# Four chunks of the first experts beside the head softmax instead of two, the projections in halves, and the openings normalized on ACT

## The chip, the cores and the metric

The kernel runs on one core of a Trainium2 chip. The metric is the device time of one execution in microseconds (us). All arithmetic is in 32-bit floating point. PE is TensorE, DVE is VectorE, ACT is ScalarE, POOL is GpSimd, and SP issues most of the DMAs.

## The reference

The input x is 2 batches of 1024 tokens of width 128. Eight residual steps follow, each `x = x + f(layernorm(x))` with its own f. The first five (a latent attention, a spiking feed-forward network, a state space, the spiking network again, a linear attention) lie ahead of the change. The last three are what matters here:

```python
x = x + experts(layernorm(x))
x = x + head_softmax_attention(layernorm(x))   # softmax over the 16 heads, not over the keys
x = x + experts(layernorm(x))

def experts(x):            # 8 experts, hidden 512, each applied to every token
    for wg, wu, wd in zip(Wg, Wu, Wd):
        acc = acc + (silu(x @ wg) * (x @ wu)) @ wd

def head_softmax_attention(x):                 # 16 heads of width 8
    dp = einsum('bhqd,bhkd->bhqk', q, k) * 8 ** -0.5
    attn = softmax(dp, axis=1)                 # axis 1 is the head
    out = einsum('bhqk,bhkd->bhqd', attn, v) @ w_proj + b_proj
```

Both expert steps use the same weights.

## The kernel before

The tokens stay in SBUF as `x_res`, 16 tiles of 128 tokens; batch 0 has tiles 0 to 7, batch 1 tiles 8 to 15. There are two forms of the experts.

- `experts_ffn(chunks)` takes chunks of 512 tokens (4 tiles). Its units, 8 experts x 4 slices of the hidden width, run as a pipeline: products (two 128x512 matmuls), gate on ACT (Silu), multiplication on DVE, and the output matmul two units later into one PSUM bank.
- `ExpertStream` takes chunks of 256 tokens (2 tiles), numbered 0 to 7, also 32 units each, and is fed step by step: `products` takes two units, `gates` applies Silu, `multiply` forms `e_h`, `outputs` multiplies two of these with `Wd` into a bank `h_pd`, and `add` adds it to `x_res`. An `opening` normalizes a chunk (statistics on DVE, root on ACT, inverse on DVE, apply, transposes on PE) and so makes its 32 units available. Two units handled by one call are called a pair below.

`heads_and_experts(first, second)` computes the attention and weaves the stream into it: the chunks `first` are still the experts ahead of the attention, and `second` those behind it. It runs under a manual schedule: each engine does its instructions in the order in which they are written.

- `preparation(b)` makes queries, keys and values of a batch, as steps that name the engine they belong to ("dve", "act", "pool", "pe").
- 128 blocks follow: for each batch, 8 query tiles x 8 key tiles of 128. A block computes the scores of all 16 heads (`products`, h_s), the maximum over the heads (DVE, h_m), the difference (DVE, h_e), the exponential (ACT), the sum over the heads (a copy of half of h_e by a DMA from SP, an accumulating DMA from POOL, and eight matmuls with the identity, h_pd), the reciprocal (DVE, h_r), the weights (POOL, h_a) and the weighted values (PE, h_po). These run skewed over several turns of one loop. The score banks (`h_s`) and `h_pd` exist once.
- In each turn the stream gives one pair: outputs, multiplication, products and gates stand at fixed places between the steps of the softmax.
- `aside(place)` does one waiting step of a side list if it belongs to that engine. A "pe" step takes the place of the products of that turn. The side list says when an opening or a preparation may start: at so many finished query tiles, and with at most so many units left.
- Ahead of the blocks, the steps of `preparation(0)` alternate with pairs of the stream's first chunk; behind the last block the rest of the stream is done alone.

At the end of the kernel the calls are

```python
    experts_ffn(g, w, [2])
    heads_and_experts(g, w, [6, 7], [0, 1, 2, 3, 4, 5])
    experts_ffn(g, w, [3])
```

Tiles 8 to 11 of batch 1 are the 512-token chunk 2, or the stream's chunks 4 and 5. `experts_ffn([3])` is the second expert step of the last four tiles.

Of the kernel before, what the change touches and what calls it, by code (L numbers as in the profile page):

```python
# [9 lines left out]
F32 = mybir.dt.float32  # L10
BF16 = mybir.dt.bfloat16
AF = mybir.ActivationFunctionType
# [7 lines left out]
P = 128  # L20
B = 2
L = 1024
D = 128
NT = B * L // P
TPB = L // P
# [975 lines left out]
class ExpertStream:  # L1001
# [5 lines left out]
    def __init__(self, g, w, work, ps):  # L1007
        self.g, self.w, self.work, self.ps = g, w, work, ps
        self.units, self.fresh, self.gated, self.ready, self.sums = [], [], [], [], []

    def tokens(self, chunk):
        return self.g.x[:, 2 * chunk : 2 * chunk + 2, :]

    def opening(self, chunk):

        g, nc = self.g, self.g.nc
        ln = StagedNorm(g, self.tokens(chunk), 2, "ex")
        u = self.work.tile([P, 2, D], F32, name="e_u", bufs=1)
        yield "dve", lambda: ln.stats(range(2))
        yield "act", ln.root  # L1020
        yield "dve", ln.inverse
        yield "pool", lambda: ln.apply(u, range(2))

        def transposes():
            pt = self.ps.tile([P, 4, P], F32, name="e_pgu")
            for t in range(2):
                nc.tensor.transpose(pt[:, t, :], u[:, t, :], g.ident)
            uT = self.work.tile([P, 2 * P], F32, name="e_uT")
            nc.scalar.copy(uT, pt[:, 0:2, :].rearrange("p a b -> p (a b)"))
            self.units += [(chunk, e, fc, uT) for e in range(self.NE) for fc in range(self.FC)]  # L1030

        yield "pe", transposes

# [58 lines left out]
def heads_and_experts(g, w, first, second):  # L1092

    nc, tc = g.nc, g.tc
    J, K, HD, H = 4, 4, 8, 16
    scale = HD**-0.5
    with ExitStack() as es:
        pool = lambda name, bufs, **kw: es.enter_context(tc.tile_pool(name=name, bufs=bufs, **kw))
        one = pool("h_one", 1)
        seq = pool("h_seq", 2)  # L1100
# [19 lines left out]
        vz = one.tile([P, TPB * J, K, K, HD], F32, name="h_vz")  # L1120
        nc.gpsimd.memset(vz, 0.0)
        ex = ExpertStream(g, w, ework, ps_e)
        qzs, kTs, vs = {}, {}, {}

        def preparation(b):

            xb = g.x[:, b * TPB : (b + 1) * TPB, :]
            ln = StagedNorm(g, xb, TPB, "h")
            u = seq.tile([P, TPB, D], F32, name="h_u", bufs=1)
            uT = seq.tile([P, L], F32, name="h_uT", bufs=1)  # L1130
            qzs[b] = seq.tile([P, K, L], F32, name="h_qz")
            kTs[b] = seq.tile([P, L], F32, name="h_kT")
            vs[b] = seq.tile([P, TPB, D], F32, name="h_v", bufs=1)
            for t in range(0, TPB, 2):
                yield "dve", lambda t=t: ln.stats((t, t + 1))
            yield "act", ln.root
            yield "dve", ln.inverse
            for t in range(0, TPB, 2):
                yield "pool", lambda t=t: ln.apply(u, (t, t + 1))


            def bias(t):
                nc.gpsimd.tensor_add(
                    xb[:, t : t + 4, :], xb[:, t : t + 4, :], w["b_proj2"].unsqueeze(1).to_broadcast([P, 4, D])
                )

            def transposes(n):
                pt = ps_e.tile([P, 4, P], F32, name="e_pgu")
                for t in range(4):
                    nc.tensor.transpose(pt[:, t, :], u[:, 4 * n + t, :], g.ident)  # L1150
                nc.scalar.copy(uT[:, bass.ts(n, 512)], pt.rearrange("p a b -> p (a b)"))

            def query(n):
                cols = bass.ts(n, 512)
                pm = ps_e.tile([P, 4, P], F32, name="e_pgu").rearrange("p a b -> p (a b)")
                nc.tensor.matmul(pm, w["w_qkv2"][:, 0:P], uT[:, cols], start=True, stop=True)
                for k in range(K):
                    nc.scalar.activation(  # L1158
                        qzs[b][:, k, cols], pm, AF.Identity, bias=keep_b[:, k : k + 1], scale=keep[:, k : k + 1]
                    )  # L1160

            def key(n):
                cols = bass.ts(n, 512)
                pm = ps_e.tile([P, 4, P], F32, name="e_pgu").rearrange("p a b -> p (a b)")
                nc.tensor.matmul(pm, w["w_qkv2"][:, P : 2 * P], uT[:, cols], start=True, stop=True)
                nc.scalar.activation(kTs[b][:, cols], pm, AF.Identity, bias=w["b_qk2"][:, 1:2])

            def value(n):
                pv = ps_e.tile([P, 4, P], F32, name="e_pgu")
                for t in range(4):  # L1170
                    nc.tensor.matmul(
                        pv[:, t, :], uT[:, bass.ts(4 * n + t, P)], w["w_qkv2"][:, 2 * P : 3 * P], start=True, stop=True
                    )
                nc.vector.tensor_add(
                    vs[b][:, 4 * n : 4 * n + 4, :], pv, w["b_v2"].unsqueeze(1).to_broadcast([P, 4, D])
                )

            for step in (transposes, key, query, value):
                for n in range(2):
                    yield "pe", lambda step=step, n=n: step(n)  # L1180
            for t in (0, 4):
                yield "pool", lambda t=t: bias(t)

        def spread(b):
            v = vs[b].rearrange("p t (j k d) -> p (t j) k d", j=J, k=K)
# [2 lines left out]

        def products(b, qb, kb):

            s = ps_s.tile([P, J, 512], F32, name="h_s")
            for j in range(J):
                quad = slice(32 * j, 32 * j + 32)
                nc.tensor.matmul(  # L1194
                    s[:, j, :].rearrange("p (k q) -> p k q", k=K),
                    kTs[b][quad, bass.ts(kb, P)],
                    qzs[b][quad, :, bass.ts(qb, P)],
                    start=True,
                    stop=True,
                )  # L1200
            return s.rearrange("p j (k q) -> p (j k) q", k=K)
# [50 lines left out]

        side = [(2 * c + 2, 8, ex.opening(c)) for c in second]
        side.insert(1, (0, 24, preparation(1)))
        side = [(0, 8, ex.opening(c)) for c in first[1:]] + side
        finished, current, head = 0, None, None

        def aside(place):  # L1260

            nonlocal current, head
            while True:
                if head is None:
                    if current is None:
# [12 lines left out]
            return True  # L1278

# [5 lines left out]
        n = len(blocks)  # L1285
        with tc.manual_schedule(engines=ALL):
            for _, step in ex.opening(first[0]):
                step()
            for place, step in preparation(0):
                step()  # L1290
                if place != "act":
                    po = ps_d.tile([P, 4, D], F32, name="h_pd")
                    ex.outputs(po)
                    ex.add()
                    ex.products()
                    ex.gates()
                    ex.multiply()
            spread(0)
            e_, e2_, d_, a_ = {}, {}, {}, {}
            oT = po = None  # L1300
# [159 lines left out]
def kernel(ctx: ExitStack, tc: tile.TileContext, d: dict, out: bass.AP):  # L1460
    g = Ctx(ctx, tc, d)
# [107 lines left out]
```

## Time and profile before

| | us |
|---|---|
| median of 3 runs | 2264.68 (2258.48 to 2269.89) |
| profiled execution | 2259.17 |
| its span, first to last instruction | 2257.5 |
| first product of experts_ffn([2]) | 1094.26 |
| first product of the stream | 1180.38 |
| first scores (h_s) | 1242.71 |
| first and last maxima (h_m) | 1243.92 and 2131.74 |
| first product of experts_ffn([3]) | 2166.05 |

The lower rows are starts, counted from the first instruction of the span. From the first to the last maxima are 127 distances between blocks. A row of the trace gives start, duration, engine, line, operation, and in brackets how long the engine stood idle ahead of it and what ended that. A matmul of 32-bit numbers appears as two records, so that "x8" is four matmuls. Line numbers of the kernel before are used unless a text says otherwise; the changed kernel's are a few lines higher or lower.

### The profile page before, as it was taken

How to read it: one execution, taken by the hardware profiler on the slowest of the kernel's cores; microseconds unless marked ns; L12 is line 12 of the kernel's file. 1: busy time of each engine (PE TensorE's matmuls, PEld its weight loads, DVE VectorE, ACT ScalarE, POOL GpSimd, SP SyncE). 2: the span in 40 equal slices, each digit the busy share in tenths (PEclk: the TensorE clock that was granted, in tenths of full speed). 3: DMA queues.
4: the chain of work that ended last, by engine and by line, in shares of the span. 5: the costliest groups of instructions: out<-in, count | busy, mean ns of one | idle time of the engine just before them, and what ended most of it. 6: DMA issues, size and time to landing. Idle time of an engine off the chain costs nothing. (4 is left out here: it accounts for less than half of the span.)

```text
span 2257.5 us, 36362 instructions
## 1 busy us (share of the span) xinstructions
PE 1975.7 (88%) x14832; PEld 1162.4 (51%) x14832; DVE 1685.4 (75%) x2030; ACT 1215.2 (54%) x1551; POOL 890.8 (39%) x464
## 2 busy tenths in 40 slices
PE   7679888889957758995898798988999999999999
PEld 4223343323334313343446576766777777777754
DVE  5966766898774699874333898988899998998822
ACT  1026512276624667744323675756777776777722
POOL 0013400063401000000101577888777777787710
PEclk9979978989988879997999899999999999999999
DMA  3000000296631386510000556555556655655500
GB/s 89 1 1 1 1 1 1 63 227 152 161 103 46 99 195 162 138 35 0 1 0 1 132 148 156 151 154 150 150 150 155 153 148 149 155 153 148 150 15 5
DMA packets 73799, 220.16 MB, mean 98 GB/s; under 512 B 9184, under 2 KB 19872, under 8 KB 73504
## 3 DMA queue, kind: packets, MB, share of 16 engines
q1 hardware_dynamic: 54736, 149.40, 22.4%
q0 software_dynamic: 18432, 67.12, 15.8%
q8 instruction: 116, 1.90, 0.4%
q10 hardware_dynamic: 464, 1.33, 0.3%
q14 instruction: 51, 0.42, 0.1%
HBM read 78.35 MB, written 5.24 MB: 37 GB/s over the span
## 5 line engine op out<-in xcount | busy, mean ns | idle before, releaser
L1239 POOL TENSOR_TENSOR h_a<-h_e,h_r 128x2048 f32<-128x2048 f32 x128 | 583.0, 4555 | 132.5 <-PE h_po L1245 92.9
L1205 DVE TENSOR_REDUCE h_m<-h_s 128x128 f32<-128x2048 f32 x128 | 293.1, 2290 | 70.3 <-PE h_s L1194 70.0
L1229 PE MATMUL h_pd<-h_e,ident 128*128 128x128 f32 x2048 | 263.4, 282 | 39.4 <-DMA h_e<-h_e 25.6
L1211 DVE TENSOR_TENSOR h_e<-h_s,h_m 128x2048 f32<-128x2048 f32 x128 | 292.4, 2284 | 2.4 <-DVE h_m L1205 0.6
L1214 ACT ACTIVATE h_e<-h_e 128x1024 f32<-128x1024 f32 x256 | 256.5, 1049 | 65.5 <-DVE h_e L1211 56.9
L1229 PEld LDWEIGHTS h_pd<-h_e,ident 128*128 128x128 f32 x2048 | 241.4, 193 | 82.3 <-DVE x_res L1078 47.2
L1050 ACT ACT_TABLE_LOAD x110 | 141.1, 1283 | 164.9 <-PE e_pgu L1043 164.6
L377 POOL TENSOR_SCALAR_AFFINE_SELECT a_pT<-a_pT 128x256 f32<-128x256 f32 x120 | 126.9, 1079 | 210.3 <-ACT a_pT L374 207.5
L279 DVE TENSOR_REDUCE a_nm<-a_s 128x2 f32<-128x1024 f32 (+7 forms) x144 | 168.1, 1216 | 43.0 <-PE a_s L270 27.6
L963 DVE TENSOR_TENSOR e_h<-e_sg,e_pu 128x512 f32<-128x512 f32 x128 | 86.5, 685 | 145.4 <-PE e_pu L956 131.4
L958 ACT ACTIVATE e_sg<-e_pg 128x512 f32<-128x512 f32 x128 | 76.4, 597 | 184.0 <-PE e_pg L955 163.9
L1069 PEld LDWEIGHTS h_pd<-Wd,e_h 128*128 128x128 f32 x1024 | 125.1, 191 | 95.0 <-DVE e_h L1058 78.8
L374 ACT ACTIVATE a_pT<-a_st 128x1024 f32<-128x1024 f32 (+3 forms) x176 | 129.9, 791 | 66.2 <-PE a_st L360 64.6
L1194 PE MATMUL h_s<-h_qz,h_kT 32*128 32x512 f32 x1024 | 147.9, 647 | 16.4 <-DVE h_e L1211 11.1
L792 DVE TENSOR_TENSOR_SCAN s_h<-s_a,s_h 128x1024 f32<-128x1024 f32 x64 | 148.8, 2325 | 18.0 <-ACT s_a L760 14.2
L1224 POOL DMA_DIRECT2D h_e<-h_e x128 | 114.9, 897 | 109.0 <-DVE h_m L1205 48.7
L1043 PE MATMUL e_pgu<-e_uT,Wg 128*128 128x256 f32 x512 | 154.9, 384 | 2.6 <-ACT h_qz L1158 2.1
L1069 PE MATMUL h_pd<-Wd,e_h 128*128 128x128 f32 x1024 | 149.7, 288 | 6.5 <-DVE e_h L1058 4.7
L261 PE MATMUL a_s<-a_latT,a_qT 32*128 32x512 f32 (+3 forms) x768 | 119.8, 602 | 40.6 <-DVE a_nm L279 38.7
L956 PE MATMUL e_pu<-e_uT,Wu 128*128 128x512 f32 x256 | 135.6, 612 | 20.3 <-DVE e_h L963 20.3
L1043 PE MATMUL e_pgu<-e_uT,Wu 128*128 128x256 f32 x512 | 153.2, 381 | 0.0
L1214 ACT ACT_TABLE_LOAD x111 | 142.4, 1283 | 12.4 <-issue 5.6
(283 smaller groups left out, 3243.2 us busy)
## 6 DMA issues: line engine op xcount, KB each, us to landing
h_e<-h_e SPq DMA_DIRECT2D x128, 512.0 KB, 4.1
h_e<-h_e POOLq DMA_DIRECT2D x128, 512.0 KB, 4.6
s_a<-s_steps SPq DMA_DIRECT2D x64, 512.0 KB, 5.0
s_h<-s_steps SPq DMA_DIRECT2D x64, 512.0 KB, 6.5
s_steps<-s_gate SPq DMA_DIRECT2D x8, 256.0 KB, 2.1
Wg<-in_Wg_dram SPq DMA_DIRECT2D x8, 256.0 KB, 5.8
Wu<-in_Wu_dram SPq DMA_DIRECT2D x8, 256.0 KB, 5.8
Wd<-in_Wd_dram SPq DMA_DIRECT2D x8, 256.0 KB, 6.0
```

The lines of the kernel that those rows point to most:

```text
L279: nc.vector.tensor_reduce(nm[:, half, i, h : h + together], s[:, :, :n], AX.X, ALU.max, negate=True)
L792: nc.vector.tensor_tensor_scan(h, a, h, 0.0, ALU.mult, ALU.add)
L956: nc.tensor.matmul(pu, w["Wu"][:, e, f], opened[n], start=True, stop=True)
L1043: nc.tensor.matmul(pgu[:, k, :], w[name][:, e, f], uT, start=True, stop=True)
L1050: nc.scalar.activation(sg, pgu[:, 0, :], AF.Silu)
L1069: nc.tensor.matmul(po[:, t, :], h[:, bass.ts(t, P)], self.w["Wd"][:, e, fc, :], start=(k == 0), stop=(k == 1))
L1194: nc.tensor.matmul(s[:, j, :].rearrange("p (k q) -> p k q", k=K), kTs[b][quad, bass.ts(kb, P)], qzs[b][quad, :, bass.ts(qb, P)], start=Tru ...
L1205: nc.vector.tensor_reduce(m, heads.rearrange("p h q -> p q h"), AX.X, ALU.max)
L1211: nc.vector.tensor_sub(e, heads, m.unsqueeze(1).to_broadcast([P, H, P]))
L1214: nc.scalar.activation(eh, eh, AF.Exp, scale=scale)
L1229: nc.tensor.matmul(pd, g.ident, e2[:, k, :], start=(k == 0), stop=(k == 7))
L1239: nc.gpsimd.tensor_mul(a, e, r.unsqueeze(1).to_broadcast([P, H, P]))
```

## The change

- `experts_ffn([2])` is gone. Its tokens become the stream's chunks 4 and 5, at the head of `first`.
- `preparation` is cut into two halves of 512 tokens, each with its own normalization, transposes, key, query, value and bias. For batch 0 both run ahead of the blocks; for batch 1 each half is its own entry in the side list.
- The normalizations of openings and preparations are applied by ACT (`apply_on_act`, one activation for each tile with a scale and a shift, and one small DVE instruction for the shift) instead of by POOL.
- A pair done outside of the blocks, with the waiting side steps ahead of it, is a function `alone`. Ahead of the blocks `alone` is called until at most 76 units of the first chunks are left, counting 32 for each chunk not yet opened. The same function empties the stream behind the last block.
- The limits at which side steps may start are larger.

```diff
-        yield "pool", lambda: ln.apply(u, range(2))
+        yield "act", lambda: ln.apply_on_act(u)
...
             self.units += [(chunk, e, fc, uT) for e in range(self.NE) for fc in range(self.FC)]
+            self.unopened = max(self.unopened - 1, 0)
...
-        def preparation(b):
+        def preparation(b, n):
-            xb = g.x[:, b * TPB : (b + 1) * TPB, :]
-            ln = StagedNorm(g, xb, TPB, "h")
+            xh = g.x[:, b * TPB + 4 * n : b * TPB + 4 * n + 4, :]
+            cols = bass.ts(n, 512)
+            ln = StagedNorm(g, xh, 4, "h")
...
-            for t in range(0, TPB, 2):
-                yield "pool", lambda t=t: ln.apply(u, (t, t + 1))
+            yield "act", lambda: ln.apply_on_act(u)
...
             for step in (transposes, key, query, value):
-                for n in range(2):
-                    yield "pe", lambda step=step, n=n: step(n)
-            for t in (0, 4):
-                yield "pool", lambda t=t: bias(t)
+                yield "pe", step
+            yield "pool", lambda: nc.gpsimd.tensor_add(
+                xh, xh, w["b_proj2"].unsqueeze(1).to_broadcast([P, 4, D])
+            )
...
-        side = [(2 * c + 2, 8, ex.opening(c)) for c in second]
-        side.insert(1, (0, 24, preparation(1)))
-        side = [(0, 8, ex.opening(c)) for c in first[1:]] + side
-        finished, current, head = 0, None, None
+        side = [(0, 28 if k else 16, ex.opening(c)) for k, c in enumerate(first[1:])]
+        side += [(0, 64, preparation(1, 0))]
+        side += [(2 * c + 2, 16 if c else 28, ex.opening(c)) for c in second]
+        side.insert(len(first) + 1, (0, 24, preparation(1, 1)))
+        finished, current, head, ex.unopened = 0, None, None, len(first)
...
+        def alone():
+            for place in ("dve", "act", "pool", "pe"):
+                aside(place)
+            po = ps_d.tile([P, 4, D], F32, name="h_pd")
+            ex.outputs(po)
+            ex.add()
+            ex.products()
+            ex.gates()
+            ex.multiply()
...
-            for place, step in preparation(0):
-                step()
-                if place != "act":
-                    po = ps_d.tile([P, 4, D], F32, name="h_pd")
-                    ex.outputs(po)
-                    ex.add()
-                    ex.products()
-                    ex.gates()
-                    ex.multiply()
+            for half in range(2):
+                for place, step in preparation(0, half):
+                    step()
+                    if place != "act":
+                        alone()
+            while len(ex.units) + 32 * ex.unopened > 76:
+                alone()
...
             while ex.units or ex.fresh or ex.gated or ex.ready or side or current:
-                while any([aside(place) for place in ("dve", "act", "pool", "pe")]):
-                    pass
-                po = ps_d.tile([P, 4, D], F32, name="h_pd")
-                ex.outputs(po)
-                ex.add()
-                ex.products()
-                ex.gates()
-                ex.multiply()
+                alone()
...
-    experts_ffn(g, w, [2])
-    heads_and_experts(g, w, [6, 7], [0, 1, 2, 3, 4, 5])
+    heads_and_experts(g, w, [4, 5, 6, 7], [0, 1, 2, 3, 4, 5])
     experts_ffn(g, w, [3])
```

More of the change, by code (lines that the diff above doesn't have):

```diff
@@ L1009, in __init__ @@
         self.units, self.fresh, self.gated, self.ready, self.sums = [], [], [], [], []
+    unopened = 0
     def tokens(self, chunk):
@@ L1122, in heads_and_experts @@
         ex = ExpertStream(g, w, ework, ps_e)
-        qzs, kTs, vs = {}, {}, {}
-        def preparation(b):
-            xb = g.x[:, b * TPB : (b + 1) * TPB, :]
-            ln = StagedNorm(g, xb, TPB, "h")
[L1129 to L1133, printed above, removed]
-            for t in range(0, TPB, 2):
+        qzs, kTs, vs, prepared = {}, {}, {}, set()
+        def preparation(b, n):
+            xh = g.x[:, b * TPB + 4 * n : b * TPB + 4 * n + 4, :]
+            cols = bass.ts(n, 512)
+            ln = StagedNorm(g, xh, 4, "h")
+            u = seq.tile([P, 4, D], F32, name="h_u", bufs=1)
+            uT = seq.tile([P, 512], F32, name="h_uT", bufs=1)
+            if n == 0:
+                qzs[b] = seq.tile([P, K, L], F32, name="h_qz")
+                kTs[b] = seq.tile([P, L], F32, name="h_kT")
+                vs[b] = seq.tile([P, TPB, D], F32, name="h_v", bufs=1)
+            for t in (0, 2):
                 yield "dve", lambda t=t: ln.stats((t, t + 1))
@@ L1137, in preparation @@
             yield "dve", ln.inverse
-            for t in range(0, TPB, 2):
-                yield "pool", lambda t=t: ln.apply(u, (t, t + 1))
[L1142 to L1147, printed above, removed]
-                pt = ps_e.tile([P, 4, P], F32, name="e_pgu")
-                for t in range(4):
-                    nc.tensor.transpose(pt[:, t, :], u[:, 4 * n + t, :], g.ident)
-                nc.scalar.copy(uT[:, bass.ts(n, 512)], pt.rearrange("p a b -> p (a b)"))
@@ L1153, in query, with project @@
[L1153 to L1156, printed above, removed]
+            yield "act", lambda: ln.apply_on_act(u)
+            def project(rows):
+                pm = ps_e.tile([P, 4, P], F32, name="e_pgu").rearrange("p a b -> p (a b)")
+                nc.tensor.matmul(pm, w["w_qkv2"][:, rows], uT, start=True, stop=True)
+                return pm
@@ L1157, in query, with transposes, key @@
+            def transposes():
+                pt = ps_e.tile([P, 4, P], F32, name="e_pgu")
+                transpose4(g, pt, u)
+                nc.scalar.copy(uT, pt.rearrange("p a b -> p (a b)"))
+            def key():
+                nc.scalar.activation(kTs[b][:, cols], project(slice(P, 2 * P)), AF.Identity, bias=w["b_qk2"][:, 1:2])
+            def query():
+                pm = project(slice(0, P))
+                qz = qzs[b][:, :, cols]
                 for k in range(K):
                     nc.scalar.activation(
-                        qzs[b][:, k, cols], pm, AF.Identity, bias=keep_b[:, k : k + 1], scale=keep[:, k : k + 1]
+                        qz[:, k, :], pm, AF.Identity, bias=keep_b[:, k : k + 1], scale=keep[:, k : k + 1]
@@ L1160, in query, with value @@
                     )
[L1162 to L1168, printed above, removed]
+            def value():
                 pv = ps_e.tile([P, 4, P], F32, name="e_pgu")
@@ L1171, in value @@
                     nc.tensor.matmul(
-                        pv[:, t, :], uT[:, bass.ts(4 * n + t, P)], w["w_qkv2"][:, 2 * P : 3 * P], start=True, stop=True
+                        pv[:, t, :], uT[:, bass.ts(t, P)], w["w_qkv2"][:, 2 * P : 3 * P], start=True, stop=True
                     )
@@ L1176, in value @@
                 )
+                prepared.add((b, n))
             for step in (transposes, key, query, value):
-                for n in range(2):
-                    yield "pe", lambda step=step, n=n: step(n)
-            for t in (0, 4):
-                yield "pool", lambda t=t: bias(t)
+                yield "pe", step
+            yield "pool", lambda: nc.gpsimd.tensor_add(
+                xh, xh, w["b_proj2"].unsqueeze(1).to_broadcast([P, 4, D])
+            )
         def spread(b):
@@ L1189, in products @@
         def products(b, qb, kb):
+            assert (b, max(qb, kb) // 4) in prepared
             s = ps_s.tile([P, J, 512], F32, name="h_s")
```

## The prediction

> **What bounds the kernel now.** I read the page first, then busy time by stage, then the order in time of one block of the head softmax, of the stretch ahead of it and of the tail.
>
> ```profile
> PE 1975.7 (88%) x14832; PEld 1162.4 (51%) x14832; DVE 1685.4 (75%) x2030; ACT 1215.2 (54%) x1551; POOL 890.8 (39%) x464
> ```
>
> PE leads over the whole span, but the change touches only four stages. By stage (PE busy, PEld, DVE, ACT, POOL, clock, DMA share):
>
> ```profile
> 1094.20:1179.40 85.20, 84.47 (x196) 37.37 (x197) 22.00 (x33) 20.98 (x35) 0.98 (x2) 0.98 0.00 0
> 1180.30:1242.70 62.40, 54.63 (x288) 42.27 (x288) 25.45 (x68) 22.94 (x48) 11.65 (x11) 1.00 0.00 1
> 1243.90:2131.70 887.80, 832.35 (x8725) 635.38 (x8725) 796.84 (x773) 630.26 (x740) 689.75 (x275) 0.99 0.59 151
> 2131.70:2166.00 34.30, 29.10 (x310) 23.91 (x310) 14.57 (x27) 13.95 (x24) 18.91 (x6) 0.99 0.29 74
> ```
>
> The first row is experts_ffn([2]): PE never stops. The second is the preparation of batch 0 with 32 expert units beside it, PE 88% busy. The third is the 128 blocks, 6.88 us each when undisturbed. The last is the drain. One block:
>
> ```profile
> 2125.72 0.60 PE L1043 MATMUL e_pgu<-e_uT,Wg 128*128 128x256 f32 x2
> ...
> 2127.07 0.41 DVE L1078 TENSOR_TENSOR x_res<-x_res,h_pd 128x256 f32<-128x256 f32 x1
> 2127.40 2.28 DVE L1211 TENSOR_TENSOR h_e<-h_s,h_m 128x2048 f32<-128x2048 f32 x1
> 2127.54 2.05 PE L1229 MATMUL h_pd<-h_e,ident 128*128 128x128 f32 x16
> ...
> 2129.63 0.96 DVE L1234 RECIPROCAL h_r<-h_pd 128x128 f32<-128x128 f32 x1
> ...
> 2130.53 1.14 PE L1194 MATMUL h_s<-h_qz,h_kT 32*128 32x512 f32 x8
> ```
>
> DVE needs 2.29 (maxima) + 0.41 + 2.28 + 0.96 + 0.69 = 6.63 of the 6.88 us, and PE about 6.8 with a pair of units. Both are full, and they hand work to each other. So a block without units is no shorter at once: in the 20 blocks where the order of the program has none, most starts of h_m still lie 6.9 us apart. A pair put into such a block is free.
>
> The same pair outside a block is not:
>
> ```profile
> 1199.54 0.60 PE L1043 MATMUL e_pgu<-e_uT,Wg 128*128 128x256 f32 x2
> ...
> 1201.47 0.38 ACT L1050 ACTIVATE e_sg<-e_pgu 128x256 f32<-128x256 f32 x1 [0.48 <-DVE e_h L1058]
> ...
> 1201.89 0.42 DVE L1058 TENSOR_TENSOR e_h<-e_sg,e_pgu 128x256 f32<-128x256 f32 x1 [0.44 <-ACT e_sg L1050]
> ...
> 1202.36 0.94 PE L1069 MATMUL h_pd<-Wd,e_h 128*128 128x128 f32 x6 [0.37 <-DVE e_h L1058]
> 1203.13 0.60 PE L1043 MATMUL e_pgu<-e_uT,Wg 128*128 128x256 f32 x2
> ```
>
> The outputs wait for the gate and product of the pair just ahead, so a pair takes 1203.13 - 1199.54 = 3.59 us. experts_ffn does the same work (one unit of 512 tokens) in 2.57.
>
> **The change part by part.** *Counting units.* In the order of the two programs: before, 32 units of 256 tokens ahead of the blocks, 214 between the first and last h_s, 10 behind, and 64 units' worth in experts_ffn([2]). After: 52 ahead, 224 between, 44 behind, none in experts_ffn. The lead thus brings only 10 more units under the softmax (15 blocks without units instead of 20); the other 54 move from dense code to the stretch ahead and the tail.
>
> *Ahead of the blocks.* Before, from the first product of experts_ffn([2]) at 1094.26 to the first h_s at 1242.71: 148.4 us. After: the opening of chunk 4 takes the place of that of experts_ffn. With two tiles instead of four (0.83 less on ACT, 0.43 on DVE, 0.21 of copy) it would be done at about 1092.7. But the memset of h_vz, 3.51 us of POOL, is now free to run as soon as POOL's last x_res row ends at 1090.44, and:
>
> ```profile
> 1179.76 3.51 POOL L1121 MEMSET h_vz<- 128x4096 f32 x1 [84.58 <-PE e_pgu L1027]
> ...
> 1180.78 2.51 DVE L1118 TENSOR_SCALAR h_keep_b<-h_keep,b_qk 128x4 f32<-128x4 f32 x1
> ```
>
> The 128x4 row took 2.51 us and ended with the memset. The Trainium skill, "SBUF — State Buffer", section "Who interferes with whom", says why: tensor_scalar can take the port pair that VectorE shares with GpSimd, and whichever starts second waits for the whole of the other. This speaks against the change, since the row now stands ahead of the shift of the first opening. By the rule the first product comes at 1093.95 + 0.15 + 0.83 + 0.4 + 0.4 = 1095.7; if the row slips in ahead of the memset, 1092.7. I take 1095.7.
>
> Then 26 pairs: 25 x 3.59 = 89.8, and 1.7 to the h_s behind the last one. Added: 1.0 for the first pair (cold clock, Silu table). For each half of the preparation 0.8 for the root (rows 1195.14 to 1199.54, 4.40 instead of 3.59), 2.3 for four applies on ACT (1.65 as in e_u L76 x4) between the last gate and the transposes, of which the old POOL rows (6.22 for 8, hidden) cost nothing, 0.2 key, 1.35 query, 0.3 value: 5.0, twice 10.0. Two openings (5 and 6) with a root 0.8 and two applies 1.4: 4.4. Sum 89.8 + 1.7 + 1.0 + 10.0 + 4.4 = 106.9; first h_s at 1202.6, 40.1 earlier. The biases stay on POOL, which is idle there. The roots rest on table loads of 1.28 with the Silu directly behind. The skill ("ScalarE: Activation LUTs", "What ACT_TABLE_LOAD costs") adds a drain of about 1.38 to each switch. In the trace no drain follows: load at 2126.83, Silu at 2128.13. By the page four roots with two switches would cost 11 more and turn the sum to a loss; I take the row.
>
> *The blocks.* 887.8 us is 127 x 6.88 = 873.8 and 14.0 more. 3.3 of that are the 16 projections (7.09 blocks), which stay. Much of the rest follows openings:
>
> ```profile
> 2023.40 1.86 POOL L82 TENSOR_SCALAR e_u<-x_res,ex_mv,ex_rs 128x128 f32<-128x128 f32 x2
> ...
> 2029.41 1.19 POOL L1224 DMA_DIRECT2D h_e<-h_e  x1
> ...
> 2050.80 2.02 PE L1229 MATMUL h_pd<-h_e,ident 128*128 128x128 f32 x16 [2.48 <-DMA h_e<-h_e]
> ```
>
> The apply delays POOL's product and so its accumulating DMA. Later blocks wait for DMA; the four or five blocks after an opening are 0.5 to 3 us longer, about 11.5 over all, and preparation(1) another 1.4. The fast start without units gave 1.7 back. After, the applies stand on ACT ahead of the gates. ACT has 1.60 idle there, but the apply must await its shift, which stands behind x_res L1078 on DVE. So the Silu load and the exponentials come 1.7 us later in that block (2.5 for the four tiles of a half). SP's copy of h_e is queued behind the exponentials, and POOL's accumulate behind that. The trace has no such delay. From below it is free, since POOL stands idle 1.5 ahead of its next product and PE's denominators come 1.4 after the usual landing. From above all of it passes on: 7 x 1.7 + 2 x 2.5 = 17. I take 0.4 an opening and 1.0 a half by those slacks: 2.8 + 2.0, and 1.2 for each query. 7.2 against 11.2: the blocks lose 4 to 6 us, say 5.
>
> *The tail.* Before: 34.3 us from the last h_m to the first product of experts_ffn([3]). After, 17 more pairs stand between. Here the chain of 3.59 does not hold: the blocks multiply a pair one block later, so two pairs stay in flight, and the outputs in the tail belong to the pair before last. PE then sets the pace: 1.73 for the products and 1.0 for outputs (2131.60 to 2132.60), 2.73. Pair 6 starts 29.1 behind the last h_m. The Sqrt and Silu loads and four applies of the last experts_ffn now fall into pairs 6 and 7, so pair 8 starts at about 35.5. 14 x 2.73 to pair 22, then 5.4 for two outputs, transposes and copy: 79.1, so 44.8 more. PE no longer rests ahead of experts_ffn([3]), whose first products came 1.7 us apart instead of 0.86 (2166.05 to 2173.52): 3.2 back. The tail gives 41.6.
>
> **Sum.** -40.1 - 5 + 41.6 = -3.5 us. The profiled execution took 2259.17 (span 2257.5), so 2255.7. It lies 5.5 below the median of 2264.68; the forecast in medians is 2261.
>
> **The rivals.**
> - *ACT becomes the late engine.* The place is the exponentials behind an opening's applies. POOL's 1.57 us came out as 1.9 a time, with echoes. If 1.7 on ACT echoes alike, 2.0 x 7 + 3.0 x 2 + 2.4 = 22.4 against 11.2: +11, sum +13, 2277. It decides once the delay exceeds the 1.5 us ahead of POOL's product. For it: POOL already waited for h_e DMAs 35 times. Against: ACT is idle 1.6 a block.
> - *The lead pays more.* No echo is left and the memset misses the first opening: -11 in the blocks, -3 ahead, 2252. For it: the POOL rows that the later DMA waits follow are gone. Against: query steps (2.78 on ACT) lengthened blocks even before.
> - *The tail keeps the 3.59 chain:* 14 x 0.86 = +12, sum +8.5, 2273. Against it is the order of the instructions.
>
> **How the numbers follow.** The main case has 0.50 (own range 2254 to 2268), ACT late 0.17, the tail chain 0.10, more gain 0.23. The terms ahead (-44 to -36), in the blocks (-11 to +11) and behind (+38 to +47) reach -17 to +22. The range 2243 to 2279 leaves out about two in ten. 0.5%, about what a measurement of this kernel can tell from no change, is 11.3 us: faster 0.24, same 0.54, slower 0.22.
>
> **What would show it.** Right: the first h_m at about 1204; pairs 3.6 apart ahead and 2.7 in the tail; the keep_b row ending with the memset; blocks of 6.88 with smaller bumps behind openings; the first experts_ffn product 79 us behind the last h_m. Wrong: waits of L1226 on h_e growing, tail pairs at 3.6, or blocks without units that get shorter.

## The result, and the profile after

The changed kernel took 2282.15 us (median of 7 runs, 2276.67 to 2288.99) against 2262.17 us (7 runs, 2253.43 to 2269.89) for the kernel before. The ratio is 1.0085 with a 95% interval of 1.0063 to 1.0107: slower by 0.85%, where 2261 us was forecast. The profiled executions stand at 2282.15 and 2259.17 us (spans 2280.4 and 2257.5). The first is the median of its kernel, the second 3 below.

The two spans, cut at the same events:

| stretch | before | after | difference | forecast |
|---|---|---|---|---|
| start to the last x_res add of the linear attention (L909) | 1087.96 | 1081.26 | -6.7 | 0 |
| to the first h_m | 155.96 | 126.86 | -29.1 | -40.1 |
| first to last h_m, the 128 blocks | 887.82 | 905.18 | +17.4 | -5 |
| last h_m to the first product of experts_ffn([3]) | 34.31 | 78.78 | +44.5 | +44.8 |
| to the end | 91.41 | 88.35 | -3.1 | -3.2 |
| sum | 2257.46 | 2280.43 | +23.0 | -3.5 |

The first line is scatter. PE's instructions up to there are the same in both kernels, and in the profiles of all kernels of this study that row starts anywhere from 1078.8 to 1088.9. So a stage length of a single execution is good to some microseconds, and small differences below are judged by the medians.

Both terms behind the blocks are right to 0.3 us. Two are wrong: the stretch ahead gave 11 us less than forecast, and the blocks lost 17 us where they were to gain 5. First the busy time of each engine over the whole span of after, from the page:

```profile
PE 1988.2 (87%) x15148; PEld 1211.7 (53%) x15148; DVE 1711.0 (75%) x2109; ACT 1249.8 (55%) x1631; POOL 868.0 (38%) x432
```

ACT has 35 us more and POOL 23 less, as the moved applies and the added loads would have it; the shares of the engines hardly move, and tell nothing of the loss. Busy time by stage of after does (length, then PE, PEld, DVE, ACT and POOL busy, granted clock, DMA share, GB/s):

```profile
1089.30:1206.90 117.60, 96.76 (x444) 75.09 (x444) 37.25 (x106) 45.51 (x90) 2.54 (x2) 0.89 0.00 1
1208.10:2113.30 905.20, 851.61 (x8821) 652.15 (x8822) 810.23 (x800) 652.48 (x781) 672.95 (x253) 0.99 0.58 147
2113.30:2192.10 78.80, 72.60 (x575) 63.93 (x575) 35.49 (x77) 27.56 (x58) 19.29 (x6) 1.00 0.15 36
2192.10:2280.40 88.30, 83.30 (x196) 36.79 (x196) 22.67 (x33) 19.69 (x33) 0.00 (x0) 0.99 0.02 5
```

The first row is the stretch from the first product of the stream to the first h_s. Its clock is 0.89; the two rows of before that it replaces had 0.98 and 1.00. In the blocks PE's busy time rose by 19 us for 96 more matmul records and DVE's by 13, without a larger share of either: what is new there is waiting. In order of time, one half of the second batch's preparation in a block of after:

```profile
1298.26 4.52 POOL L1241 TENSOR_TENSOR h_a<-h_e,h_r 128x2048 f32<-128x2048 f32 x1 [0.98 <-PE h_po L1247]
...
1301.41 0.41 DVE L1082 TENSOR_TENSOR x_res<-x_res,h_pd 128x256 f32<-128x256 f32 x1
1301.74 1.06 DVE L74 SCALAR_TENSOR_TENSOR h_nb<-h_mv,h_rs 128x4 f32<-128x4 f32 x1
...
1302.72 2.28 DVE L1213 TENSOR_TENSOR h_e<-h_s,h_m 128x2048 f32<-128x2048 f32 x1
...
1302.84 1.65 ACT L76 ACTIVATE h_u<-x_res,h_nb,h_rs 128x128 f32<-128x128 f32 x4 [3.29 <-DVE h_nb L74]
1304.51 1.28 ACT L1054 ACT_TABLE_LOAD   x1
1305.80 0.66 ACT L1054 ACTIVATE e_sg<-e_pgu 128x256 f32<-128x256 f32 x2
...
1307.77 2.00 ACT L1216 ACTIVATE h_e<-h_e 128x1024 f32<-128x1024 f32 x2
...
1312.31 0.88 POOL L1226 DMA_DIRECT2D h_e<-h_e  x1 [1.73 <-DMA h_e<-h_e]
```

The shift L74 (in the bracket behind a row stands the idle time before it and what ended it) is a DVE row of 128x4 elements. It takes 1.06 us and ends within 0.02 us of POOL's product L1241, at 1302.78. ACT has stood idle for 3.29 us when the shift comes. Then follow the applies, the Silu load, the gate and the Exp load, and the exponentials start 5.05 us behind the start of DVE's difference h_e. In an undisturbed block of after it is 2.70, so the delay is 2.35 us, close to the 2.5 that the prediction gave it. POOL next waits for the copy of h_e. In the waits of after, the line that says how long POOL stood for that (us in sum, count, longest; 45.4, 37, 2.8 before):

```profile
POOL h_e L1226 <- DMA h_e<-h_e: 68.5, 51, 7.2
```

Growing waits of this kind were the first sign of being wrong that the prediction had named. The seven blocks from this half on take 54.3 us instead of the 48.2 of undisturbed ones, and the seven from the other half on 54.3 as well. Behind an opening it can be the like. In block 92, which takes 11.03 us, PE rests and then runs its denominators at half clock (3.76 us instead of 2.02). It is not so each time: in lag2 below, which has the same order there, this block takes 7.85 us.

```profile
1866.46 0.80 PE L1324 MATMUL h_pd<-w_proj,h_oT 128*128 128x128 f32 x2 [1.92 <-ACT h_oT L1355]
1868.02 3.76 PE L1231 MATMUL h_pd<-h_e,ident 128*128 128x128 f32 x16 [0.33 <-PE e_pgu L1030]
```

Now ahead of the blocks, an opening of after in order of time, and the clock of the 6.8 us behind it:

```profile
1132.93 0.88 ACT L76 ACTIVATE e_u<-x_res,ex_nb,ex_rs 128x128 f32<-128x128 f32 x2 [1.60 <-DVE ex_nb L74]
1133.48 0.86 PE L1030 MATMUL e_pgu<-ident,e_u 128*128 128x128 f32 x2 [3.33 <-ACT e_u L76]
1134.13 1.91 PE L1073 MATMUL h_pd<-Wd,e_h 128*128 128x128 f32 x8
```
```profile
1132.60:1139.40 6.80, 5.92 (x19) 5.00 (x20) 1.10 (x5) 1.63 (x4) 0.00 (x0) 0.50 0.00 0
```

PE rests 3.33 us for root, inverse, shift and applies, and afterwards has a granted clock of 0.50: the outputs L1073 take 1.91 us, and 1.05 at full clock. The transposes of the two halves and of the other opening have shorter rests ahead of them, 2.39, 2.34 and 2.53 us, and each is followed by 3.4 us at half clock as well. The first of them, and the clock behind it:

```profile
1104.85 1.63 PE L132 MATMUL e_pgu<-ident,h_u 128*128 128x128 f32 x4 [2.39 <-ACT h_u L76]
```
```profile
1105.32:1108.70 3.38, 3.38 (x13) 2.85 (x14) 0.42 (x1) 1.21 (x3) 1.27 (x1) 0.50 0.00 0
```

The stretch starts cold too (0.50 in its first 9.2 us). The keep_b row waited for the memset as forecast, and the first opening's shift stands behind it:

```profile
1083.80 3.51 POOL L1125 MEMSET h_vz<- 128x4096 f32 x1
1084.27 3.06 DVE L1122 TENSOR_SCALAR h_keep_b<-h_keep,b_qk 128x4 f32<-128x4 f32 x1
1084.41 2.92 DVE L74 SCALAR_TENSOR_TENSOR ex_nb<-ex_mv,ex_rs 128x2 f32<-128x2 f32 x1
```

### The profile page after: what moved, and what is told of

Read it like the earlier page. It is cut to its first block, busy times and chain, and to the rows that moved or that the text cites. A ratio compares the mean times of both kernels' runs of the same rounds, so it can differ in the third digit from the quotient of the medians.

```text
span 2280.4 us, 37135 instructions
## 1 busy us (share of the span) xinstructions
PE 1988.2 (87%) x15148; PEld 1211.7 (53%) x15148; DVE 1711.0 (75%) x2109; ACT 1249.8 (55%) x1631; POOL 868.0 (38%) x432
## 5 line engine op out<-in xcount | busy, mean ns | idle before, releaser
L1241 POOL TENSOR_TENSOR h_a<-h_e,h_r 128x2048 f32<-128x2048 f32 x128 | 581.1, 4540 | 137.1 <-PE h_po L1247 86.7
L1073 PEld LDWEIGHTS h_pd<-Wd,e_h 128*128 128x128 f32 x1280 | 162.9, 196 | 106.0 <-DVE e_h L1062 84.5
L1047 PE MATMUL e_pgu<-e_uT,Wg 128*128 128x256 f32 x640 | 197.0, 390 | 4.5 <-ACT h_qz L1163 2.2
L1073 PE MATMUL h_pd<-Wd,e_h 128*128 128x128 f32 x1280 | 190.8, 291 | 8.1 <-DVE e_h L1062 6.4
L1047 PE MATMUL e_pgu<-e_uT,Wu 128*128 128x256 f32 x640 | 194.0, 385 | 0.0
L1062 DVE TENSOR_TENSOR e_h<-e_sg,e_pgu 128x256 f32<-128x256 f32 x320 | 116.4, 395 | 72.8 <-ACT e_sg L1054 72.8
L1054 ACT ACTIVATE e_sg<-e_pgu 128x256 f32<-128x256 f32 x320 | 110.0, 381 | 106.5 <-PE e_pgu L1047 92.1
L1236 DVE RECIPROCAL h_r<-h_pd 128x128 f32<-128x128 f32 x128 | 121.8, 952 | 32.7 <-PE h_pd L1231 32.2
```

What stands on the lines that cost most here:

```text
L1047: nc.tensor.matmul(pgu[:, k, :], w[name][:, e, f], uT, start=True, stop=True)
L1054: nc.scalar.activation(sg, pgu[:, 0, :], AF.Silu)
L1073: nc.tensor.matmul(po[:, t, :], h[:, bass.ts(t, P)], self.w["Wd"][:, e, fc, :], start=(k == 0), stop=(k == 1))
L1241: nc.gpsimd.tensor_mul(a, e, r.unsqueeze(1).to_broadcast([P, H, P]))
```

## The experiments

The theory after the result: *the change loses by the place of its applies.* The shift is formed on DVE at the step that uses it, late in a block; ACT waits for it with the exponentials queued behind, and ahead of the blocks PE rests meanwhile and loses its clock. Lead, halves and tail cost in sum what the forecast said. The rival: *the lead itself costs it*, since 54 units moved out of dense code into stretches that run at 3.59 us a pair or worse.

In each table line below, "ahead" is from the first product of the stream to the first h_s, "blocks" from the first to the last h_m, "tail" from there to the first product of experts_ffn([3]), each from one profiled execution. Medians are of 10 runs, of 7 for after and of 4 for mult_ahead and combo_pool. Ratios are to the kernel before, run beside it, and need not be the quotient of two medians. The two kernels made from before (before_act, before_lag2) are not in the table, since their stretches begin elsewhere.

| kernel | median us | ratio (95%) | ahead | blocks | tail |
|---|---|---|---|---|---|
| after | 2282.15 | 1.0085 (1.0063 to 1.0107) | 117.6 | 905.2 | 78.8 |
| pool_all | 2260.54 | 1.0012 (0.9994 to 1.0030) | 108.8 | 891.3 | 77.1 |
| shift_early | 2264.03 | 1.0023 (1.0004 to 1.0042) | 113.9 | 890.8 | 77.2 |
| late_dummy | 2266.32 | 1.0020 (0.9998 to 1.0041) | 113.8 | 894.4 | 77.2 |
| mult_ahead | 2285.76 | 1.0137 (1.0092 to 1.0181) | 103.8 | 900.6 | 97.9 |
| lag2 | 2265.02 | 1.0022 (1.0000 to 1.0044) | 100.3 | 897.4 | 80.4 |
| lead_none | 2275.37 | 1.0067 (1.0045 to 1.0090) | 73.3 | 898.7 | 111.3 |
| combo_pool | 2242.65 | 0.9918 (0.9888 to 0.9948) | 94.6 | 884.4 | 80.3 |
| combo_shift | 2253.85 | 0.9969 (0.9955 to 0.9983) | 97.7 | 887.7 | 80.5 |
| combo_lead | 2250.92 | 0.9960 (0.9943 to 0.9977) | 78.7 | 896.8 | 94.4 |

How far a single profile can be trusted in the blocks shows where kernels run the same code there. Before and before_lag2 took 887.8 and 891.2 us; after, lag2 and mult_ahead took 905.2, 897.4 and 900.6. The profile of after is the slowest of its three, so a loss read from it alone is more likely too large than too small.

**pool_all: after, with the applies of openings and preparation on POOL.** Lead and halves stay.

```diff
-        yield "act", lambda: ln.apply_on_act(u)            # opening
+        yield "pool", lambda: ln.apply(u, range(2))
-            yield "act", lambda: ln.apply_on_act(u)        # preparation
+            for t in (0, 2):
+                yield "pool", lambda t=t: ln.apply(u, (t, t + 1))
```

> The changed kernel with the openings and the half preparations normalized on POOL again, all else as changed. Theory 1 (the applies on ACT are the loss: they push the exponentials in the blocks, and ahead of the blocks they stand between gate and transposes and let PE rest until its clock drops): the blocks, first to last maxima, go from 905.2 us to about 890, the stretch from the first product to the first scores from 117.6 to about 107, the whole to about 2258. Theory 2 (the loss is in the halves and in where the units lie, whoever applies): POOL brings its own late DMAs back, blocks above 900, the whole within 5 us of 2282.

Measured: 1.0012, no difference from before that can be measured. The lead, the halves and the tail in sum cost nothing, so the rival falls; the whole 0.73% (1.0085 less 1.0012, some 16.5 us) lies in where the applies stand. It is a net sum: the 3.59 chain in it costs, as lag2 shows, and the forecast had priced it. The halves were not tried by themselves. Busy time by stage, ahead and in the blocks:

```profile
1094.10:1203.00 108.90, 89.52 (x446) 69.63 (x446) 36.75 (x102) 40.53 (x78) 11.95 (x14) 0.95 0.00 1
1204.20:2095.50 891.30, 848.63 (x8821) 650.97 (x8822) 800.84 (x792) 643.47 (x759) 690.10 (x275) 0.99 0.58 150
```

For nearly the same matmuls ahead (446 and 444 recorded) PE is busy 89.5 us instead of 96.8, at a clock of 0.95 instead of 0.89; that is 7.2 of the 8.7 us that the stretch gets shorter. Not all of the clock can be put down to the applies. After a rest of nearly the same length ahead of the stretch (6.87 us here, 6.72 in after) 4.0 us of the stretch start cold here and 9.2 in after. Behind the halves it is the applies: here the rest is 1.40 us, and the clock behind it stays at 1.00 where after had 0.50.

```profile
1106.52 1.26 PE L1073 MATMUL h_pd<-Wd,e_h 128*128 128x128 f32 x8 [1.40 <-DVE e_h L1062]
```
```profile
1106.50:1110.00 3.50, 3.42 (x18) 2.70 (x18) 1.17 (x4) 0.77 (x2) 1.77 (x2) 1.00 0.00 0
```

The blocks get 13.9 shorter.

**shift_early: after, with the shift formed one step earlier, with the inverse.** The applies stay on ACT. The edit is the same for openings and preparation:

```diff
-        yield "dve", ln.inverse
-        yield "act", lambda: ln.apply_on_act(u)
+        yield "dve", ln.inverse_and_shift     # reciprocal, then the shift
+        yield "act", lambda: ln.apply_shifted(u)
```

> The changed kernel, applies on ACT, but the shift is formed on DVE together with the inverse, one step earlier, so that the apply no longer waits for a DVE instruction that stands behind the maxima and beside POOL's product. Theory 1a (the apply is late because of its shift): the exponentials behind an apply are late by under 1 us instead of 1.7 to 3.3, blocks about 892, whole about 2268. Theory 1b (ACT has no room for the applies, shift or not): blocks within 4 us of 905, whole about 2280. Theory 2 (halves and placing): the same as 1b.

Measured: 1.0023, blocks 890.8. One instruction of 128x2 or 128x4 moved by one step takes 14 us out of the blocks by the two profiles, and 0.62% out of the whole, which is some 14 us too; 3.7 of them stand ahead of the blocks and 1.5 in the tail, so that some 9 are left for the blocks. The half preparation above, now in order of time:

```profile
1295.89 0.16 DVE L83 SCALAR_TENSOR_TENSOR h_nb<-h_mv,h_rs 128x4 f32<-128x4 f32 x1
...
1298.29 1.63 ACT L87 ACTIVATE h_u<-x_res,h_nb,h_rs 128x128 f32<-128x128 f32 x4
...
1300.36 2.28 DVE L1224 TENSOR_TENSOR h_e<-h_s,h_m 128x2048 f32<-128x2048 f32 x1
...
1301.59 0.88 POOL L1237 DMA_DIRECT2D h_e<-h_e  x1
...
1303.20 2.01 ACT L1227 ACTIVATE h_e<-h_e 128x1024 f32<-128x1024 f32 x2
```

The shift takes 0.16 us, before POOL's product begins. The applies start with no wait ahead of them, before the difference instead of behind it, and the exponentials follow the difference by 2.84 us instead of 5.05. So it is not ACT's work that lengthened the blocks (652.0 us here, 652.5 in after) but the moment at which it was let go. The seven blocks from each half on take 51.7 and 50.8 us here instead of 54.3 twice, so the late shift cost some 3 us a half. Ahead of the blocks the stretch is 113.9: there the early shift gives 3.7 us and POOL's applies 8.7.

**late_dummy: shift_early, with the shift formed once more at the old place, into a tile that nothing reads.** Does DVE lose the time, or ACT?

```diff
     def apply_shifted(self, dst):
+        again = self.g.small.tile([P, self.nt], F32, name=f"{self.key}_again", bufs=2)
+        self.g.nc.vector.scalar_tensor_tensor(again, self.mv[:, :, 0], -1.0, self.rs, ALU.mult, ALU.mult)
```

> The kernel shift_early (applies on ACT, shift formed with the inverse) with one instruction more: where the changed kernel forms the shift, DVE forms it again into a tile that nobody reads. The DVE stall beside POOL's product is back, ACT's wait for it is not. If the loss in the blocks was DVE's own stall (row of 1.06 us where 0.15 is its work), the blocks take about 900 us or more again, the whole about 2275. If it was ACT waiting and the exponentials being late, the blocks stay near 891 and the whole near 2265.

Measured: 1.0020 and 894.4 in the blocks. The groups of the shift in late_dummy (the idle copy) and in shift_early (the one that is used), duration in ns (least, median, most):

```profile
L87 DVE SCALAR_TENSOR_TENSOR ex_again<-ex_mv,ex_rs x10: 153/1156/2855, 1090.8 to 2093.2; 128x2 f32<-128x2 f32 x10
```
```profile
L83 DVE SCALAR_TENSOR_TENSOR ex_nb<-ex_mv,ex_rs x10: 141/160/2923, 1088.1 to 2083.3; 128x2 f32<-128x2 f32 x10
```

The copy at the old place takes 1.16 us in the median, the early one 0.16. So DVE does stall, but that alone costs 3.6 us in the blocks by the profile, which is no more than their scatter, and nothing by the ratios (1.0020 and 1.0023). The larger part of the loss comes from ACT waiting for the result with the gate and the exponentials behind it.

**before_act: the kernel before, with the applies on ACT and the shift late.** No lead, no halves. Here the shift is written over the mean.

```diff
-        yield "pool", lambda: ln.apply(u, range(2))        # opening
+        yield "act", lambda: ln.apply_in_place(u)
-            for t in range(0, TPB, 2):                     # preparation
-                yield "pool", lambda t=t: ln.apply(u, (t, t + 1))
+            yield "act", lambda: ln.apply_in_place(u)
```

> The kernel before with nothing changed but the applies of openings and preparation, which go to ACT (the shift formed in place, one DVE instruction at the place where the changed kernel has it). Theory 1: blocks from 887.8 us to about 900 (seven openings and one preparation of eight tiles), the stretch of the preparation 3 to 5 us longer, the whole 2274 to 2280. Theory 2: within 4 us of the kernel before, or faster, since POOL's late DMAs behind openings (11 us in the forecast) are gone.

Measured: 2262.58, 1.0019 (1.0000 to 1.0038). In its profile the blocks are 12.4 longer (900.3), as the first theory had it, but the whole costs 0 to 9 us, where that theory wanted 12 or more; 2.6 us above before is what the second theory named. So this run alone would not have shown the cause. Put beside pool_all this sizes the loss: of after's 16.5 us the profile puts 8.7 ahead of the blocks, a stretch in which before_act lost nothing (60.6 us, and 62.3 in before). That leaves some 8 for the blocks, within what before_act allows. By single profiles the same share is 13.9. So the blocks' part lies between 8 and 14 us; these runs don't say closer.

**mult_ahead: after, with the multiply of the pair before put ahead of the products in the pairs done alone.** It was to test whether the 3.59 chain is a matter of order.

```diff
-            for place in ("dve", "act", "pool", "pe"):
+            for place in ("dve", "act", "pool"):
                 aside(place)
             po = ps_d.tile([P, 4, D], F32, name="h_pd")
             ex.outputs(po)
             ex.add()
+            ex.multiply()
+            aside("pe")
             ex.products()
             ex.gates()
-            ex.multiply()
...
                 for place, step in preparation(0, half):
+                    if place == "pe":
+                        ex.multiply()
                     step()
```

> The changed kernel with the multiplication of the pair before moved ahead of the products in the pairs done alone, as it stands in the blocks, so that two pairs are in flight ahead of the blocks. If the chain products, gate, multiplication, outputs sets the 3.59 us of a pair there, pairs take about 2.7 us and the stretch from first product to first scores falls from 117.6 to about 97, the whole to about 2262. If the two banks of products set it, or the PE clock, pairs stay above 3.3 us and the whole above 2276.

Measured: 2285.76, 1.0137, pairs 3.73 apart both ahead and in the tail. The tail in order of time:

```profile
2148.33 0.42 DVE L1082 TENSOR_TENSOR x_res<-x_res,h_pd 128x256 f32<-128x256 f32 x1 [2.65 <-PE h_pd L1073]
2148.66 0.74 DVE L1062 TENSOR_TENSOR e_h<-e_sg,e_pgu 128x256 f32<-128x256 f32 x2
2149.13 0.48 PE L1047 MATMUL e_pgu<-e_uT,Wg 128*128 128x256 f32 x1 [0.84 <-DVE e_h L1062]
```

The multiply stands behind the add on DVE, the add waits for the outputs, and the next products wait for the multiply's buffer. The edit swapped one chain for another. As a test of the order it is a miss, and says nothing against the idea. It does bear on the stretch ahead, which is 13.8 us shorter than in after (103.8) though its pairs are slower: the longest PE rests in it are 2.13 and 2.21 us, its clock is 0.98, and the applies stand on ACT with the late shift as before. That speaks for the rests and the clock, not for ACT's work, as what costs ahead of the blocks.

**lag2: after, with the outputs held back until more than two pairs are ready.**

```diff
-            ex.outputs(po)
+            if len(ex.ready) > 2 or not (ex.units or side or current):
+                ex.outputs(po)
```

> The changed kernel where a pair done alone gives its outputs only when two pairs are multiplied, so that the outputs always belong to the pair before last, ahead of the blocks as in the tail; the order of products, gates and multiplication stays. If the 3.59 us of a pair ahead of the blocks is the chain through gate and multiplication, pairs take the tail's 2.62 there, the stretch from first product to first scores falls from 117.6 to about 95, and the whole to about 2260. If the stretch is held by the applies and the cold clock, it stays above 110 and the whole above 2275.

Measured: 1.0022, 0.63% below after, and 100.3 ahead. Pairs ahead of the blocks in order of time:

```profile
1161.82 0.60 PE L1047 MATMUL e_pgu<-e_uT,Wg 128*128 128x256 f32 x2
1163.55 1.05 PE L1073 MATMUL h_pd<-Wd,e_h 128*128 128x128 f32 x8
1164.44 0.60 PE L1047 MATMUL e_pgu<-e_uT,Wg 128*128 128x256 f32 x2
```

1164.44 - 1161.82 = 2.62 us, the pace of the tail, where 3.59 was the pace with the outputs of the pair just ahead. The prediction's reading of the chain, and of why the tail is free of it, is thus shown. The blocks are 897.4 with the late shift still there; by the profiles 17.3 us of the gain stand ahead of them.

**before_lag2: the same edit in the kernel before**, beside the preparation of batch 0.

```diff
-                    ex.outputs(po)
+                    if len(ex.ready) > 2 or not ex.units:
+                        ex.outputs(po)
```

> The kernel before with only the outputs given two pairs late beside the preparation of batch 0, as in lag2. 16 pairs there, of which some 10 at 3.59 us would go to 2.6 or 2.9: 8 to 12 us less, about 2250. If the gain needs the changed kernel's longer stretch, within 3 us of before.

Measured: 2254.79, 0.9978 (0.9961 to 0.9995); the stretch goes from 62.3 to 56.0 us. 16 pairs by 0.97 would be 15.5, and 8 to 12 were expected; 6.3 were won. In its profile the last five distances between pairs stay as they were in before, at 3.81 to 4.9 us.

**lead_none: after, with no chunk in the lead** (limit 96 instead of 76): 32 units ahead, 64 in the tail.

> The changed kernel with the limit of the lead at 96 units instead of 76, so that no pair is done ahead of the blocks beyond the 16 beside the preparation; by the order of the program 20 units move from ahead of the blocks to the tail, and as many blocks as before (15) have none. If the units in the blocks are set by the later chunks and not by the lead, ten pairs go from 3.59 to 2.62 us and one opening leaves the stretch ahead: about 12 us less, 2270. If the lead fills blocks, the time grows by up to 10 us.

Measured: 2275.37, about 7 us below after by the medians and 4 by the ratios, whose intervals lie over each other, so that a gain is not shown. In the profile, which is of the fastest of the ten runs, the tail takes 111.3 (+32.5) and the stretch ahead 73.3 (-44.3): the 20 units and their opening, which also moves to the tail, are 12 us dearer ahead. Ten pairs by 0.97 are 9.7 of that. As after is built, with the 3.59 chain, the units of the lead lie on the dearer side of the blocks.

**combo_pool: pool_all and lag2 together, and the memset of h_vz issued behind the first opening.**

```diff
-        nc.gpsimd.memset(vz, 0.0)
 ...
             for _, step in ex.opening(first[0]):
                 step()
+            nc.gpsimd.memset(vz, 0.0)
```

> Applies on POOL as in the first experiment, outputs two pairs late as in lag2, and the memset of h_vz behind the first opening, so that the 128x4 row no longer waits for it. The gains should add up if they are separate: 2260.5 less about 22 for the pairs and 3 for the memset, about 2236, below the kernel before. If the stretch ahead is held elsewhere, above 2250.

Measured: 2242.65, 0.9918 (0.9888 to 0.9948), faster than both kernels: 0.8% below before, 1.7% below after. By stage (ahead, blocks, tail), and then the keep_b row:

```profile
1087.30:1181.90 94.60, 83.01 (x436) 69.07 (x436) 35.82 (x101) 40.52 (x78) 14.44 (x15) 0.93 0.00 1
1183.10:2067.50 884.40, 845.27 (x8829) 648.35 (x8830) 801.49 (x793) 643.26 (x759) 690.48 (x275) 0.99 0.59 151
2067.50:2147.80 80.30, 74.10 (x574) 65.21 (x574) 35.79 (x77) 27.94 (x59) 18.74 (x6) 0.98 0.12 30
```
```profile
1084.67 0.21 DVE L1122 TENSOR_SCALAR h_keep_b<-h_keep,b_qk 128x4 f32<-128x4 f32 x1
```

Keep_b takes 0.21 us instead of 3.06, and from the start of the last x_res add of the linear attention to the first product it is 5.8 us instead of 8.06. The stretch ahead is 23 us shorter than in after, the blocks 21.

**combo_shift: shift_early, lag2 and the late memset.**

> As the kernel with POOL's applies, outputs two pairs late and the memset behind the first opening, but with the applies on ACT and the shift formed with the inverse. About 2240, some 4 us above the POOL form, as it was in the first experiments.

Measured: 2253.85, 14 above what was expected. Ahead it is 97.7, 3.1 more than combo_pool, and from the last add to the first product 8.07, so the late memset gained nothing there. The trace says why: with the applies on ACT, POOL has nothing to do in the opening, and the memset written behind it starts as early as before.

```profile
1089.23 3.51 POOL L1316 MEMSET h_vz<- 128x4096 f32 x1
1089.70 3.06 DVE L1133 TENSOR_SCALAR h_keep_b<-h_keep,b_qk 128x4 f32<-128x4 f32 x1
```

With these three changes POOL is the better place for the applies (0.9918 against 0.9969) even with the shift early; some 2 us of that are the memset, by the profiles.

**combo_lead: combo_pool with no chunk in the lead** (limit 96). The order of the program then has 40 units ahead, 54 in the tail, and 14 blocks without units.

> combo_pool with the limit of the lead at 96. Pairs ahead and in the tail now both take 2.62 us, so moving 20 units between them should give nothing, but one opening (about 5 us of POOL's applies between pairs) moves into the blocks: 2238 to 2243. If the lead is worth anything by itself, slower than combo_pool by over 5 us.

Measured: 2250.92, 0.4% above combo_pool, or some 8 us where 0 was expected; over 5 us was to mean that the lead is worth something by itself. Ahead and tail together are 1.8 us shorter, as the units at nearly one price let expect; the blocks are 12.4 longer, which was not expected and stays open. So with the applies on POOL and the chain gone the lead seems to pay (the two intervals just touch), and why is not known.

## Why the prediction was wrong

*Wrong: the blocks.* The step that failed is "I take 0.4 an opening and 1.0 a half by those slacks". The delay itself was right: the exponentials behind a half were to be 2.5 us late and were 2.35. What failed is the claim that POOL's and PE's slacks swallow most of it. By the profiles of after and shift_early the late shift cost some 3 us a half, and what is left of the 14 us is 1.2 for each of the seven openings. That is the upper end: the blocks' whole loss to the applies lies between 8 and 14 us. The slack was measured in undisturbed blocks, and here POOL waited 68.5 us for its copies instead of 45.4. The small row that all hung on was priced at nothing: it stands behind x_res L1082 on DVE and beside POOL's h_a product, and takes about 1.1 us instead of 0.16. The mechanism is that of the prediction's own slower rival, "ACT becomes the late engine", which got 0.17. It named +11 in the blocks; by the profile they gave +17.4. It also argued that a delay above 1.5 us decides, and took the delay to be 1.7 to 2.5: by its own threshold it should have been the likeliest case. shift_early shows the place of the shift as the cause, and late_dummy that the waiting on ACT weighs more than DVE's stall.

The other half of that sum, 11.2 us to be gained by taking POOL's applies away, did not come either: with the shift early, and with the applies back on POOL, the blocks take the same 891 us. One line on which it rested was misread. The wait of 2.48 us at 2050.80, shown as what follows an opening, stands in block 115, and in 11 of the 13 kernels PE waits 2.5 to 2.6 us for the same copy there. In after the nearest opening ahead of it lies 50 us back:

```profile
2031.80 2.02 PE L1231 MATMUL h_pd<-h_e,ident 128*128 128x128 f32 x16 [2.52 <-DMA h_e<-h_e]
```

*Wrong: the stretch ahead.* "Sum 89.8 + 1.7 + 1.0 + 10.0 + 4.4 = 106.9" measured 117.6. The pairs and the way to the h_s held. The mis-sized terms can be read from the distances between the first products of pairs, as far as they are above 3.59: the first pair and the one behind it added 4.1 us for 1.0 (they ran in the cold start), the two halves 12.4 for 10.0, and the two openings 9.5 for 4.4. The sum counted the rest that a step brings, at durations from rows of before at a granted clock of 1.00; after ran at 0.89, with 3.4 to 6.8 us at half clock behind each rest of a half or an opening. The Trainium skill, "TensorE: Matmul & The Clock Gate", section "HAM oscillation — how this bites in real kernels", warns of PE gaps over some 3.4 us. The rest of 3.33 us comes near that, but those of 2.34 to 2.53 us were followed by half clock too, while 2.13 and 2.21 in mult_ahead were not. No single length decides it here.

What the place of the applies changes ahead of the blocks is the halves. In pool_all the same reading gives 1.9 for the first pair, 5.3 for the halves and 10.1 for the openings: an opening is no cheaper with POOL. So it is luck that the stretch of pool_all, 108.8, comes within 2 us of the forecast. The forecast has 7.4 us of applies on ACT in it (2.3 a half and 1.4 an opening) which pool_all does not make.

*Right: the tail.* 79.1 and 78.8. Pairs 2.62 us apart (2.73 forecast), since outputs belong to the pair before last; lag2 shows the same pace where that order is brought in, and 3.59 where it is not. The rival that kept the chain in the tail falls.

*Right: experts_ffn([3]) starts warm*, -3.2 and -3.1; the count of the units (52, 224 and 44, 15 blocks without); keep_b waiting for the memset (3.06 us); and no drain behind the table loads: the load at 1304.51 takes 1.28 and the gate starts at 1305.80.

*Near by luck: that the halves and the lead are worth about nothing.* pool_all's 1.0012 (-1.4 to +6.8 us) comes near the sum of -3.5 us, though its interval does not hold it. But that kernel was not the one forecast, and the terms ahead and in the blocks that meet there were off one by one.

The range of 2243 to 2279 missed by 3 us. It held the +11 of the blocks or the error ahead, not both: the two were treated as independent, though both come from the applies on ACT. Nor does it fit the prediction's own terms, which it says reach from -17 to +22: added to 2264.68 that is 2248 to 2287, and 2282 lies within.

## What to carry to other kernels

Form a norm's small per-token terms as soon as their inputs exist, not at the step that uses them: late in a full block a 0.16 us row can last as long as the POOL product beside it, and what waits for it holds its whole queue. When a normalization moves to another engine, ask how long TensorE rests meanwhile, and price the work behind that rest at the clock it will have. In a stream written out serially, let the outputs belong to the pair before last (2.62 us instead of 3.59) before deciding on which side of a full stage the work should lie.

## What the hardware showed that was not expected

A DVE row with two inputs in SBUF and 2 to 4 elements a partition took 0.84 to 1.43 us in the blocks of after, each of the nine times ending within 0.03 us of a POOL product, and 0.16 us without one; the prediction knew such waiting only of keep_b and the memset. A rest of 3.33 us on PE cost half the clock for 6.8 us, and rests of 2.34 to 2.53 us for 3.4 us, so that four matmuls of 128x128 (x8 in the row) took 1.91 us instead of 1.05. And the same block, number 115, took 9 to 11 us in 12 of the 13 kernels here, far from any step that was changed; its cause stays open.
